# Masks turned by DMA instead of TensorE in a four-layer graph network: twelve in the first stage, ten among the sums

## The chip, the cores and the metric

The kernel runs on one core of a Trainium2 chip. The metric is the device time of one execution in microseconds (us). The time before is 2909.86 us, the median of three runs (2909.22 to 2911.19).

## The reference, cut to what matters

Four graph layers follow one another over N = 2708 nodes with 512 features each; every layer ends in a residual and a layer norm. All use the same adjacency matrix `adj` (2708 x 2708, int32, 0 or 1, symmetric by construction, with ones on the diagonal). The change touches only layer 0 and the way in which the adjacency comes into memory:

```python
Ab = A > 0
keep = Ab & (jnp.cumsum(Ab.astype(jnp.int32), axis=1) <= 64)    # first 64 neighbours of each row
nb_mean = (keep @ X) / jnp.maximum(keep.sum(axis=1), 1.0)
xj = jax.nn.leaky_relu(nb_mean @ W_nb.T + b_nb)
xi = jax.nn.leaky_relu(X @ W_line.T + b_line)
x = layernorm(x + xi + jnp.where(cnt > 0, xj, 0))
```

Layer 1 uses the whole mask instead of the first 64 neighbours (`mask @ x / deg`), layers 2 and 3 are attention with the same mask.

## The kernel before, in words

The rows are cut into NT = 22 tiles of P = 128; the last one has only `few` = 20 rows. One matrix `maskT` (128 x 22 x 2816, fp8, in on-chip memory) holds the transposed mask for all four layers. Each entry is a sign: 0 is no neighbour, one sign is a neighbour that is kept, the other a neighbour past the 64th.

**How one mask tile is made.** A "mask" is a block of 128 rows of `adj`. Its steps are:

- *load* (L270-L273): GpSimd (POOL) issues a DMA that reads 128 rows of int32 and writes bf16 into a tile `m`.
- *count* (L275-L277): one ScalarE (ACT) instruction over 2708 columns, with the row sum in `cnts`.
- *place* (L279-L286): VectorE (DVE) runs a scan along the row (L283) and multiplies (L286), in two halves in the first stage and in four quarters later.
- *turn*: the block is transposed. Before, there are two ways. `turn_here` (L288-L304) does it on TensorE (PE), in 22 transposes (L295) into PSUM, read by ACT as signs into `maskT` (L299). `turn` (L306-L307) does it by one DMA transpose, issued by SyncE (SP), into a bf16 tile `into`, which ACT reads as *signs* (L309-L315). Both end with a small DMA of the last rows, issued by POOL (L302, L314).

**The first stage** (L320-L369) loops over the 22 row tiles of x. For each tile PE multiplies by W_nb (the product called A here, `product` with `wnT`, L346), transposes the next tile of x into PSUM (L133), and multiplies by W_line (the product called B, L361). `keep_y` (L230) takes A apart: ACT copies the high half to `yH` (L231) and DVE subtracts for the low half `yL` (L236). B gets its bias (L363), a leaky ReLU (L195) and goes to memory by a POOL DMA (L365). ACT copies the transposed x out of PSUM (`xT`, L135); both products of the next tile need this copy. Product B has one PSUM buffer, which is free again when L363 has read it. Of the 22 masks, HERE = 14 are made in this stage (L265). The rule in L354 spreads them over the tiles from tile 2 on. They are loaded one ahead into three buffers `m` (L337). Their transposes go to PE in the written order: L350 puts the turn of a mask behind the next transposes of x. The order of PE in this stage is written out by hand (`pe`, L104); the other engines' instructions are put in order by the scheduler of the framework, which works with priorities, `issue_after` and its own estimates of time.

**The sums** (L373-L532) multiply the kept mask with `yH` and `yL`. The output tiles are taken in six blocks (two tiles, then five times four), and each block goes through 22 groups of PE instructions (L516), one for each j. ACT makes the operand `kT` of each group from `maskT` (L380), in two buffers. Behind each group one *step* of a generator is taken (L522). It runs through three parts: `other_masks` (L383) makes the remaining 8 masks, `weights1` the weights of layer 1, `vectors` those of the attention layers (L481). In `other_masks` a mask takes 11 steps: count, two empty ones, four quarters of place, at which the signs of the mask before are also made, two empty ones, then the turn and three more. The masks lie in two buffers, `spare` and `w`, which are zeroed and loaded one ahead (L389), and are turned into `weight2`. The layer norms of a finished block (`finish`, L430) run beside the groups of the next, on `rows` that SP loads. The 132 groups take 132 steps, the rest is run behind the loop (L531).

**Memory.** `yH` and `yL` (L212-L213) hold all 22 tiles of y in one piece each (128 x 22 x 512, fp32).

Of the kernel before, what the change touches and what calls it, by code (L numbers as in the profile page):

```python
# [2 lines left out]

# [6 lines left out]
F32 = mybir.dt.float32  # L10
F32R = mybir.dt.float32r
BF16 = mybir.dt.bfloat16
# [18 lines left out]
def kernel(  # L31
# [18 lines left out]
    def rows(t):  # L50
        return min(P, N - t * P)
# [151 lines left out]
    with ExitStack() as phase:  # L203
# [5 lines left out]
        gate = yp.tile([P, 1], F32, name="gate")  # L209
        nc.vector.memset(gate, -STEP / 2)  # L210
        weight2 = yp.tile([P, KD, D], F32, name="weight2")
        yH = yp.tile([P, NT, D], F32R, name="yH")  # L212
        yL = yp.tile([P, NT, D], F32R, name="yL")  # L213
        nc.gpsimd.memset(yH[:, NT - 1, :].bitcast(F32), 0.0)
        nc.gpsimd.memset(yL[:, NT - 1, :].bitcast(F32), 0.0)

        ps_tr = phase.enter_context(tc.tile_pool(name="ps_tr", bufs=2, space=PSUM))
        ps_mm = phase.enter_context(tc.tile_pool(name="ps_mm", bufs=1, space=PSUM))
# [9 lines left out]
        highs = {}  # L228

        def keep_y(t, n, pm):  # L230
            highs[t] = nc.scalar.copy(yH[:n, t, :], pm[:n])  # L231
            if t == LAST:
                low = slice(TWIN, TWIN + n)
                nc.scalar.copy(yL[low, t, :], pm[low])
                return nc.vector.tensor_sub(yH[low, t, :], pm[low], yL[low, t, :].bitcast(F32))
            return nc.vector.tensor_sub(yL[:n, t, :], pm[:n], yH[:n, t, :].bitcast(F32))  # L236

        def halves(j):

# [22 lines left out]

        HERE = NT - 8  # L265
        cuts = [(b, min(b + 4, NT)) for b in range(0, NT, 4)]
        cuts = cuts[-1:] + cuts[:-1]
        turns = [t for b in cuts for t in range(*b)]
# [10 lines left out]
        def place(i, m, places, part, of):  # L279
# [4 lines left out]
                                         places[:n, c0 - N * (part - 1) // of - 1:][:, :1] if part else -KEEP - 0.5,  # L284
                                         OP.add, OP.min)
            return nc.vector.tensor_mul(m[:n, c0:c1], m[:n, c0:c1], places[:n, :c1 - c0])  # L286

        def turn_here(i, m, psum, order=as_it_comes):  # L288
            t, n = turns[i], rows(turns[i])
            for g0 in range(0, NT, G):  # L290
                g1 = min(g0 + G, NT)
                ps = psum()
                for j in range(g0, g1):
                    w = rows(j)
                    order(nc.tensor.transpose(ps[:w, j - g0, :n], m[:n, j * P:j * P + w], identb[:n, :n]))  # L295
                parts = [(P, g0, min(g1, FULL))] + ([(rows(FULL), FULL, NT)] if g1 > FULL else [])
                for w, a, b in parts:
                    if a < b:
                        nc.scalar.activation(maskT[:w, a:b, t * P:t * P + n], ps[:w, a - g0:b - g0, :n], AF.Sign,  # L299
                                             saturate=False)  # L300
                if g1 == NT:
                    nc.gpsimd.dma_start(maskT[TWIN:TWIN + few, LAST, t * P:t * P + n],  # L302
                                        maskT[:few, LAST, t * P:t * P + n])
                yield  # L304

        def turn(i, m, into):  # L306
            nc.sync.dma_start_transpose(into, m)  # L307
# [12 lines left out]
        with ExitStack() as ph:  # L320
            st = ph.enter_context(tc.tile_pool(name="l0a", bufs=1))
            wnT, wlT = weight(), weight2
            room = [maskT[:, G + k, :4 * D].bitcast(F32) for k in range(2 * KD)]

            xs = rows_of(x)
            xTs = early(0, NT, lambda t, order=as_it_comes: transposed(ahead, ps_tr, xs(t), rows(t), "xT", order))

            transpose_weight(room[:KD], ps_tr, wnT, l0_w_nb, (nc.sync, nc.scalar))  # L330
            lows = {}
            for t in range(2):
                xT = xTs(t, order=pe)
                lows[t] = keep_y(t, P, product(xT, P, wnT, 0, pe))
            transpose_weight(room[KD:], ps_tr, wlT, l0_w_line)
            b_line = bias(bcast(l0_b_line, D))
            masks = early(1, HERE, lambda i: load_mask(i, st.tile([P, N], BF16, name="m", bufs=3)))  # L337
            masks(0)
            nc.gpsimd.memset(maskT[:, NT - 1, :], 0.0)
            nc.gpsimd.memset(maskT[:, :, N:], 0.0)  # L340
            counted = turned = 0
            for t in range(NT):
                n = rows(t)
                if t > 1:

                    lows[t] = keep_y(t, n, product(xTs(t, order=pe), n, wnT, 0, pe, sums() if t % 2 else None))  # L346
                xT = xTs(t)
                if t + 1 < NT:
                    xTs(t + 1, order=pe)
                while turned < counted - (t + 2 < NT):  # L350
                    for _ in turn_here(turned, masks(turned), lambda: sums(BF16, (P, G, P)), pe):
                        pass
                    turned += 1
                now = counted < min(HERE, -(-(t - 1) * HERE // (NT - 5)))  # L354
                if now:
                    m, places = masks(counted), st.tile([P, N // 2], BF16, name="places", bufs=1)
                    with tc.issue_after(highs[t].ins):
# [12 lines left out]

        with ExitStack() as ph:  # L373
# [9 lines left out]
            def other_masks():  # L383

                def room(i):
                    r = (ahead.tile([P, 2 * KD * (D + 2 * H)], BF16, name="w", tag="w", bufs=1) if i % 2 else
                         st.tile([P, 2 * KD * D], BF16, name="spare", tag="spare"))
                    m = r[:, :NT * P]
                    nc.gpsimd.memset(m[:, N:], 0.0)  # L389
                    load_mask(i, m)  # L390
                    return m, r[:, NT * P:NT * P + N // 4 + 1]

                got, left = {HERE: room(HERE)}, iter(())
                into = weight2.rearrange("p k c -> p (k c)").bitcast(BF16)[:, :NT * P].rearrange("p (t n) -> p t n", n=P)
                for i in range(HERE, NT):
                    if i + 1 < NT:
                        got[i + 1] = room(i + 1)
                    m, places = got.pop(i)
                    if i == HERE:
                        for _ in range(5):  # L400
                            yield
# [10 lines left out]
                    yield  # L412
# [93 lines left out]
            for i, b in enumerate(cuts):  # L506
                ts_ = range(*b)
                pa = {t: sums() for t in ts_}
                for j in range(NT):
                    if j + 1 < NT:  # L510
                        nxt, nxt_made = kept(b, j + 1)
                    elif i + 1 < len(cuts):
                        nxt, nxt_made = kept(cuts[i + 1], 0)
                    for t in ts_:
                        for y in halves(j):
                            nc.tensor.matmul(pa[t], kT[:, (t - b[0]) * P:(t - b[0] + 1) * P], y[:, j, :],  # L516
                                             start=(j == 0 and y is yH), stop=(j == LAST))
# [36 lines left out]
        with ExitStack() as ph:  # L554
            st = ph.enter_context(tc.tile_pool(name="l1b", bufs=2))
            for t in range(NT):
# [4 lines left out]
                for g0 in range(0, NT, G):  # L561
# [2 lines left out]
                    nc.scalar.copy(mf[:, :g1 - g0, :], maskT[:, g0:g1, t * P:(t + 1) * P])  # L564
                    for j in range(g0, g1):
                        for y in halves(j):
                            nc.tensor.matmul(pa, mf[:, j - g0, :], y[:, j, :],  # L567
                                             start=(j == 0 and y is yH), stop=(j == LAST))
                u = sm.tile([P, D], F32, name="u")
                nc.vector.scalar_tensor_tensor(u[:n], pa[:n], rdeg[:n, t:t + 1], z1, op0=OP.mult, op1=OP.add)  # L570
# [957 lines left out]
```

## Time and profile before

| What | Value |
|---|---|
| median of three runs | 2909.86 us |
| profiled execution, its own time | 2911.22 us |
| its span, first to last instruction | 2909.0 us |
| mean granted TensorE clock | 0.996 |
| DVE, ACT, POOL busy over the span | 68%, 52%, 9% |
| first stage, to the last product B (starts 203.25 us) | about 207 us |
| sums, to the last group of L516 (starts 467.97 us) | about 261 us |
| PE busy from 24 to 204 us, and from 204 to 468 us | 172.04 of 180, 255.87 of 264 us |

In the page and in the answers of the trace a line such as `L283 DVE TENSOR_TENSOR_SCAN` names the line of the kernel, the engine and the operation; then come the output and inputs, the shape and the number of instructions. A timeline line begins with the start and the length in us; in square brackets it has the time for which the engine stood idle before it, and what it waited for. A line with x8 is a run of eight instructions merged: an fp32 product of four matmuls shows as eight. Products overlap, so their pace is read from their starts.

### The profile page before, as it was taken

To read this page: it belongs to the slowest core of one execution; us is meant where nothing else is said; L and a number is where in the kernel's file an instruction comes from. 1 tells how busy PE (TensorE), PEld (TensorE's weight loads), DVE (VectorE), ACT (ScalarE), POOL (GpSimd) and SP (SyncE) were. 2 spreads that over 40 slices of the span, in tenths; PEclk is the share of its full clock that TensorE was granted. 3 is DMA by queue.
4 is the path that set the end of the run, shared out by engine and by line. 5 is a ranking of instruction groups with operands and counts; after the bars stand their busy time and mean duration, and the time that the engine had idled before them with its cause. 6 is when DMAs were issued, how large, how long until landed. Compare 5 with 4: busy or idle time off the path is not lost. (4 is left out here: it accounts for less than half of the span.)

```text
span 2909.0 us, 36145 instructions
## 1 busy us (share of the span) xinstructions
PE 2827.0 (97%) x14194; PEld 1576.5 (54%) x14194; DVE 1983.5 (68%) x2341; ACT 1501.7 (52%) x1749; POOL 247.5 (9%) x395
## 2 busy tenths in 40 slices
PE   8999999999999999999999999999999999999997
PEld 4457766458887434444466433444375555555555
DVE  6966737442334999999978999999954435435342
ACT  3546632122323999999955999999950000000001
POOL 1111110101110000000022000000200010100001
PEclk9999999999999999999999999999999999999999
DMA  5635536322222011111153111110171000000000
GB/s 134 129 86 121 139 110 176 112 65 93 77 75 78 27 37 37 35 46 47 34 155 107 37 37 40 47 45 34 35 179 42 4 29 11 26 15 16 15 22 21
DMA packets 145301, 187.33 MB, mean 64 GB/s; under 512 B 65791, under 2 KB 90692, under 8 KB 145122
## 3 DMA queue, kind: packets, MB, share of 16 engines
q1 hardware_dynamic: 115254, 123.27, 14.5%
q0 software_dynamic: 18864, 57.45, 7.0%
q10 hardware_dynamic: 11004, 4.22, 0.6%
q8 instruction: 114, 1.87, 0.3%
q14 instruction: 65, 0.53, 0.1%
HBM read 148.91 MB, written 44.65 MB: 67 GB/s over the span
## 5 line engine op out<-in xcount | busy, mean ns | idle before, releaser
L772 DVE SCALAR_TENSOR_TENSOR e<-v_bc,ucol,maskT 128x1408 f32<-128x1408 f32 (+3 forms) x804 | 1133.4, 1472 | 320.2 <-PE pn L1155 312.1
L801 ACT ACTIVATE c<-e,bcol 128x1300 fp8e4<-128x1300 f32 (+2 forms) x688 | 956.6, 1412 | 61.9 <-DVE e L772 16.7
L973 PE MATMUL po<-e,R 128*64 128x512 f32 (+3 forms) x4224 | 893.7, 548 | 25.9 <-DVE e L772 23.8
L973 PEld LDWEIGHTS po<-e,R 128*64 128x64 f32 (+1 forms) x4224 | 333.8, 136 | 552.7 <-issue 389.9
L1155 PE MATMUL pn<-e,R 128*128 128x512 f32 (+3 forms) x1056 | 403.0, 545 | 1.1 <-DVE lin L1175 0.4
L1155 PEld LDWEIGHTS pn<-e,R 128*128 128x128 f32 (+1 forms) x1056 | 183.9, 190 | 197.1 <-issue 181.5
L1105 ACT ACTIVATE w<-pl,b 128x256 f32<-128x256 f32 (+1 forms) x88 | 41.0, 466 | 370.9 <-PE pl L1103 370.9
L516 PE MATMUL acc<-yH,kT 128*128 128x512 f32 x484 | 194.5, 407 | 8.1 <-ACT kT L380 6.0
L567 PE MATMUL acc<-yH,mf 128*128 128x512 f32 x484 | 185.0, 389 | 0.0
L516 PE MATMUL acc<-yL,kT 128*128 128x512 f32 x462 | 181.1, 392 | 0.0
L567 PE MATMUL acc<-yL,mf 128*128 128x512 f32 x462 | 179.7, 389 | 0.0
L122 POOL TENSOR_TENSOR ln_rs<-ln_rs,half 128x1 f32<-128x1 f32 (+1 forms) x88 | 55.4, 630 | 1340.9 <-DVE ln_rs L121 1334.1
L694 PE MATMUL pm<-w,xT 128*128 128x264 f32 (+1 forms) x704 | 165.2, 388 | 2.8 <-DVE R L712 1.2
L259 PE MATMUL pm<-weight,xT 128*128 128x512 f32 (+1 forms) x344 | 156.7, 598 | 9.4 <-DVE u L363 8.0
L1103 PE MATMUL pl<-lin 128*128 128x256 f32 (+1 forms) x704 | 155.9, 376 | 3.4 <-DVE lin L1002 3.4
L1128 PE MATMUL pl<-lin,w 128*128 128x512 f32 x336 | 150.8, 593 | 0.0
L1103 PEld LDWEIGHTS pl<-lin 128*128 128x128 f32 x704 | 131.2, 193 | 34.6 <-issue 15.8
L694 PEld LDWEIGHTS pm<-w,xT 128*128 128x128 f32 (+1 forms) x704 | 129.7, 190 | 25.7 <-ACT xT L135 3.5
L564 ACT CAST mf<-maskT 128x1024 fp32r<-128x1024 fp8e4 (+1 forms) x66 | 64.5, 977 | 151.5 <-PE acc L567 148.2
L259 PE MATMUL pm<-w,xT 128*128 128x512 f32 x296 | 133.4, 593 | 3.3 <-ACT xT L135 2.1
L380 ACT ACTIVATE kT<-maskT 128x512 fp32r<-128x512 fp8e4 (+1 forms) x132 | 77.7, 593 | 103.8 <-PE acc L516 102.1
L873 PE MATMUL pd<-c,parts_c 128*12 128x384 fp8e4 (+2 forms) x2688 | 128.3, 307 | 0.0
(250 smaller groups left out, 2629.1 us busy)
## 6 DMA issues: line engine op xcount, KB each, us to landing
rows<-x_dram SPq DMA_DIRECT2D x63, 256.0 KB
v_bc<-v_dram SPq DMA_DIRECT2D x16, 704.0 KB
rows<-in_x_dram SPq DMA_DIRECT2D x42, 256.0 KB
x_dram<-u POOLq DMA_DIRECT2D x42, 256.0 KB, 2.4
v_bc<-v_dram SPq DMA_DIRECT2D x16, 650.0 KB
m<-in_adj_dram POOLq DMA_DIRECT2D x13, 677.0 KB, 7.1
r_dram<-u POOLq DMA_DIRECT2D x21, 256.0 KB, 2.3
rows<-r_dram SPq DMA_DIRECT2D x21, 256.0 KB
```

The lines of the kernel that those rows point to most:

```text
L259: order(nc.tensor.matmul(pm[:m], xT[:, k, :m], w[:, k, :], start=(k == 0), stop=(k == KD - 1)))
L380: made = nc.scalar.activation(kT[:, :w], maskT[:, j, b[0] * P:b[0] * P + w], AF.Relu, scale=-1.0)
L516: nc.tensor.matmul(pa[t], kT[:, (t - b[0]) * P:(t - b[0] + 1) * P], y[:, j, :], start=(j == 0 and y is yH), stop=(j == LAST))
L567: nc.tensor.matmul(pa, mf[:, j - g0, :], y[:, j, :], start=(j == 0 and y is yH), stop=(j == LAST))
L694: nc.tensor.matmul(pm[a][:m, :D // 2 + heads], xT[:, k, :m], w[:, k, a, :D // 2 + heads], start=(k == 0), stop=(k == KD - 1))
L772: self.made = nc.vector.scalar_tensor_tensor(e[:, :w], v[:, :w], ucol[:, j, h:h + 1], maskT[:, j, c0:c0 + w], op0=OP.max, op1=OP.mult)
L801: nc.scalar.activation(c[:, :w], e[:, :w], AF.Sigmoid, bias=bcol[:, j, h:h + 1], scale=STEP, saturate=False)
L873: pe(nc.tensor.matmul(p[32 * g:32 * g + 12, :c1 - c0], parts_c[:, j, h, :], c[:, c0:c1], start=(i == 0 and h == hs[0]), stop=(i == NT - 1 ...
L973: pe(nc.tensor.matmul(po[i][HO * k:HO * k + HO, :c1 - c0], R2[at, j, h * HO:(h + 1) * HO], e[at, a:a + c1 - c0], start=(i_ == 0), stop=(i_ ...
L1103: nc.tensor.matmul(pl[:, :w], self.lin1[:, k, f * P:(f + 1) * P], h[:, k, :w], start=(k == 0), stop=(k == KD - 1))
L1128: nc.tensor.matmul(pl[:n], gT[:, f, (t - t0) * P:(t - t0) * P + n], self.lin2[:, f, :], start=(f == 0), stop=(f == KF - 1))
L1155: nc.tensor.matmul(pn[k][:, :w], R2[at, j, k * P:(k + 1) * P], e[at, :w], start=(j == 0), stop=(j == NT - 1))
```

## The change

The change has five parts.

1. `turn_here` goes. All masks are turned by DMA transposes from SP, and ACT reads the signs from the bf16 tile that the DMA wrote.
2. HERE is 12 instead of 14: two masks move from the first stage to the sums, which now make ten.
3. The tiles into which the first ten masks of the first stage are turned lie in memory that y needs only at the end: `yH` and `yL` hold tiles 0 to 18 in one piece, and tiles 19 to 21 lie in a pair of tiles `end`. Until tile 19 these serve as two buffers for turned masks; before y is written there, the signs of the first ten must have been read. The last two masks are turned into the third buffer of `m` and the one after it.
4. The mask tiles are 2816 columns wide instead of 2708, with the tail (for the short mask the whole tile) zeroed by POOL before each load. The turn of a mask is written behind the transposes of x of the next tile, and the signs of a mask at the end of an iteration, when the next mask has been turned.
5. Among the sums the two empty steps ahead of the turn go: nine steps for a mask instead of eleven.

```diff
-        yH = yp.tile([P, NT, D], F32R, name="yH")
-        yL = yp.tile([P, NT, D], F32R, name="yL")
-        nc.gpsimd.memset(yH[:, NT - 1, :].bitcast(F32), 0.0)
-        nc.gpsimd.memset(yL[:, NT - 1, :].bitcast(F32), 0.0)
+        END = NT - 3
+        starts, ends = [yp.tile([P, END, D], F32R, name=name) for name in ("yH", "yL")], []
+
+        def end_tile(dtype):
+            return yp.tile([P, 3 * D * 4 // mybir.dt.size(dtype)], dtype, name="end", tag="end", bufs=2)
+
+        def part_of(i, t):
+            return starts[i][:, t, :] if t < END else ends[i][:, (t - END) * D:(t - END + 1) * D]
+
+        yH, yL = (partial(part_of, i) for i in range(2))
...
-        HERE = NT - 8
+        HERE = NT - 10
...
-        def turn_here(i, m, psum, order=as_it_comes):
...
-            masks = early(1, HERE, lambda i: load_mask(i, st.tile([P, N], BF16, name="m", bufs=3)))
+            def mask_tile():
+                return st.tile([P, NT * P], BF16, name="m", bufs=3)
+
+            def mask_rows(i):
+                m = mask_tile()
+                nc.gpsimd.memset(m[:, N:], 0.0)
+                if rows(turns[i]) < P:
+                    nc.gpsimd.memset(m, 0.0)
+                return load_mask(i, m)
+
+            def turned_tile(i):
+                if i >= HERE - 2:
+                    return mask_tile().rearrange("p (t n) -> p t n", n=P)
+                return end_tile(BF16)[:, :NT * P].rearrange("p (t n) -> p t n", n=P)
+
+            masks = early(1, HERE, mask_rows)
+            intos = {}
+
+            def turn_next(i):
+                intos[i] = turned_tile(i)
+                turn(i, masks(i), intos[i])
+
+            def signs_of(i):
+                for _ in signs(i, intos.pop(i)):
+                    pass
...
-            counted = turned = 0
+            counted = turned = signed = 0
             for t in range(NT):
                 n = rows(t)
+                if t == END:
+                    while signed < HERE - 2:
+                        signs_of(signed)
+                        signed += 1
+                    ends[:] = [end_tile(F32R) for _ in range(2)]
+                    for y in (yH, yL):
+                        nc.gpsimd.memset(y(LAST).bitcast(F32), 0.0)
...
-                while turned < counted - (t + 2 < NT):
-                    for _ in turn_here(turned, masks(turned), lambda: sums(BF16, (P, G, P)), pe):
-                        pass
+                while turned < counted:
+                    turn_next(turned)
                     turned += 1
...
                     counted += 1
+                while signed < (HERE if t == NT - 1 else turned - 1):
+                    signs_of(signed)
+                    signed += 1
...
                     for _ in left:
                         pass
-                    yield
-                    yield
                     turn(i, m, into)
```

The other lines of the diff only write `yH(t)` for `yH[:, t, :]` and the like.

More of the change, by code (lines that the diff above doesn't have):

```diff
@@ L1 @@
 from contextlib import ExitStack, nullcontext
+from functools import partial
 from itertools import chain
@@ L230, in keep_y @@
         def keep_y(t, n, pm):
-            highs[t] = nc.scalar.copy(yH[:n, t, :], pm[:n])
+            highs[t] = nc.scalar.copy(yH(t)[:n], pm[:n])
             if t == LAST:
                 low = slice(TWIN, TWIN + n)
-                nc.scalar.copy(yL[low, t, :], pm[low])
-                return nc.vector.tensor_sub(yH[low, t, :], pm[low], yL[low, t, :].bitcast(F32))
-            return nc.vector.tensor_sub(yL[:n, t, :], pm[:n], yH[:n, t, :].bitcast(F32))
+                nc.scalar.copy(yL(t)[low], pm[low])
+                return nc.vector.tensor_sub(yH(t)[low], pm[low], yL(t)[low].bitcast(F32))
+            return nc.vector.tensor_sub(yL(t)[:n], pm[:n], yH(t)[:n].bitcast(F32))
         def halves(j):
@@ L286, in place @@
             return nc.vector.tensor_mul(m[:n, c0:c1], m[:n, c0:c1], places[:n, :c1 - c0])
-        def turn_here(i, m, psum, order=as_it_comes):
[L289 to L303, printed above, removed]
-                yield
         def turn(i, m, into):
@@ L410, in other_masks @@
                         pass
-                    yield
-                    yield
                     turn(i, m, into)
@@ L515 @@
                         for y in halves(j):
-                            nc.tensor.matmul(pa[t], kT[:, (t - b[0]) * P:(t - b[0] + 1) * P], y[:, j, :],
+                            nc.tensor.matmul(pa[t], kT[:, (t - b[0]) * P:(t - b[0] + 1) * P], y(j),
                                              start=(j == 0 and y is yH), stop=(j == LAST))
@@ L566 @@
                         for y in halves(j):
-                            nc.tensor.matmul(pa, mf[:, j - g0, :], y[:, j, :],
+                            nc.tensor.matmul(pa, mf[:, j - g0, :], y(j),
                                              start=(j == 0 and y is yH), stop=(j == LAST))
```

## The prediction

> **What bounds the kernel now.** I read the page's busy times, then a table of the stages' windows, then the timeline of one tile of the first stage and of one mask among the sums, and last the waits of both stretches. The page says that TensorE (PE) is busy nearly throughout, so time taken off PE should come off the end, and time in which PE waits is added to it:
>
> ```profile
> span 2909.0 us, 36145 instructions
> PE 2827.0 (97%) x14194; PEld 1576.5 (54%) x14194; DVE 1983.5 (68%) x2341; ACT 1501.7 (52%) x1749; POOL 247.5 (9%) x395
> ```
>
> The change touches only the first 500 us. In the table of windows the columns are start:end, length, then busy us of PE, weight loads, VectorE (DVE), ScalarE (ACT) and GpSimd, granted clock, DMA share and GB/s:
>
> ```profile
> core 0: us, PE busy (x) PEld busy (x) DVE busy (x) ACT busy (x) POOL busy (x), PEclk, DMA share, GB/s
> 100.00:120.00 20.00, 19.46 (x90) 10.31 (x89) 19.76 (x19) 13.95 (x18) 3.63 (x6) 1.00 0.62 125
> ...
> 320.00:360.00 40.00, 38.93 (x168) 30.66 (x166) 30.48 (x53) 25.61 (x37) 8.03 (x12) 1.00 0.57 153
> ```
>
> In the first stage, in a stretch with a mask in every tile, PE and DVE are both full: less PE work alone can win little there. Among the sums PE alone is full. One tile of the first stage:
>
> ```profile
> 101.56 3.60 PE L259 MATMUL pm<-w,xT 128*128 128x512 f32 x8
> ...
> 102.23 2.95 DVE L283 TENSOR_TENSOR_SCAN places<-m,over 128x1354 bf16<-128x1354 bf16 x1
> ...
> 105.19 0.59 ACT L231 CAST yH<-pm 128x512 fp32r<-128x512 f32 x1 [2.66 <-PE pm L259]
> ...
> 105.43 1.49 PE L295 MATMUL acc<-identb,m 128*128 128x128 bf16 x22
> ...
> 105.68 0.59 ACT L135 COPY xT<-ps_tr 128x512 f32<-128x512 f32 x1
> ...
> 106.17 2.55 ACT L277 ACTIVATE m<-m,gate 128x2708 bf16<-128x2708 bf16 x1
> ...
> 106.85 3.70 PE L259 MATMUL pm<-weight,xT 128*128 128x512 f32 x8
> ...
> 108.71 2.64 ACT L299 ACTIVATE maskT<-acc 128x1024 fp8e4<-128x1024 bf16 x4
> ```
>
> PE's starts give the tile: product with W_nb 3.43 (to 104.99), transpose of x 0.44, a mask's 22 transposes 1.42, product with W_line 3.54; 8.83 in all, 7.4 without the mask. ACT's order is: high half of y, xT, count, and the signs, whose PE transposes are long done. And a mask among the sums:
>
> ```profile
> 223.71 3.48 SPq L307 DMA_TRANSPOSE weight<-spare  x1
> ...
> 229.02 1.06 ACT L312 ACTIVATE maskT<-weight 128x1024 fp8e4<-128x1024 bf16 x1 [2.09 <-DMA weight<-spare]
> ...
> 229.13 0.19 POOL L389 MEMSET spare<- 128x108 bf16 x1 [19.99 <-DMA weight<-spare]
> ...
> 230.43 0.50 PE L516 MATMUL acc<-yH,kT 128*128 128x512 f32 x1 [1.62 <-ACT kT L380]
> ```
>
> This is the pattern that decides. The transpose takes 5.3 us from its issue (223.71) to landing (229.0); ACT came to its signs 2.09 us too early and stood; the kT that PE needs lay behind, and PE lost 1.62 us.
>
> **What the Trainium skill says.** "PSUM — Partial Sum Buffer", Engine vs sequencer instructions: the queues of ScalarE, VectorE and GpSimd are strictly first in, first out. The trace agrees: the kT of 230 was held by a sign that it doesn't need. "VectorE: DVE Perf Modes", The three transpose paths: a 128x128 bf16 block costs 390 ns on TensorE and 1309 ns by DMA. In bulk both are cheaper here, 1.49/22 = 0.07 us and 5.3/22 = 0.24 us, but DMA stays the slower by 3.5 times. "DMA: Bandwidth & Descriptors", Issuing engines are not separate DMA queues: all DMAs interleave on the same 16 engines. The eight transposes agree: seven landed after 5.2 to 5.4 us, the one issued at 317.51, with row loads behind it, after 7.1.
>
> **The change, part by part.** I use the order of instructions on each engine in the built kernel, and durations from this profile.
>
> *PE transposes out of the first stage:* 13 x 1.42 + 0.75 (the 20-row mask) = 19.2 us off PE. *Two masks moved to the sums:* 2 x (2.95 + 0.86 + 3.03 + 0.87) = 15.4 us off DVE here; there 2 x 4 x (1.63 + 0.51) = 17.1 us, beside DVE's slack (30.5 of 40 busy), so nothing by itself, but 2 x 2.5 us of count in ACT's queue, each of which cost PE 0.21 among four-tile sums (six waits of PE on "ACT kT" after 245 us): 0.4.
>
> *The new wait.* Twelve masks now fall to tiles 2,3,4 | 6,7 | 9,10,11 | 13,14 | 16,17. In the built ACT order the first one or two sign groups of each mask stand ahead of the high half and xT of a following tile. After the last mask of each group they also stand ahead of the next group's first count. So sign of the last mask -> high, xT, count -> DVE's scans of the next group -> DMA transpose -> sign is one closed chain, with PE's next product behind xT. Its price: two sign groups 1.75, high 0.5, xT 0.5, count 2.55 and its 0.19 read: 5.5. The first mask on DVE: scan 2.98, product 0.79, scan 3.07, product 0.79, with leaky and subtraction (0.61 + 0.60) between: 8.9. Each further one 9.0 (the same with the addition, 0.72). Issue to landing 5.35. So 28.8 us for a group of two and 37.8 for three, where PE alone would want 3 x 7.4 = 22.2 and 4 x 7.4 = 29.6. In the profile of before mask 2 leaves DVE at 67.5; turned by DMA it lands at 72.9, and from there 28.8 + 37.8 + 28.8 + 28.8 = 124.2 brings the last sign of the stage to 197.1. Behind it: signs, high and xT 2.8, two W_nb products, one W_line product and transposes 11.3, so PE would begin the last W_line product at 211.2, against 203.25 now: **+7.9**. The saving of 19.2 is inside this: it turns into PE waiting.
>
> Each us on a landing counts five times. A mask load (677 KB, 6.1 to 7 us to land) now starts when a transpose lands and reaches into the next one: +0 to +1.75 each (5.35 to 7.1), I take 0.2: **+1**.
>
> *SP's queue:* ten transposes, 3.3 us of SP each, wait for DVE ahead of x's row loads; three row buffers give each load two tiles, some 15 us: nothing, else up to 3 us once or twice. *Memory of the end tiles:* signs of mask 9 must be read before y of tile 19 is written; that is some 20 us ahead: nothing. *Zeroing (L389's like):* 12 x 0.19 us and one of 2.5 on idle GpSimd: nothing.
>
> *Nine steps for eleven among the sums.* A step is one group of PE (1.82 us for four tiles). From a mask's count to its first sign lay 13 steps: 326.90 to 351.58 = 24.7 us. The removed two leave 11: 20.4. From count to landing the eight masks took 17.4, 17.3, 20.5, 16.9, 23.3, 18.7, 24.7, 16.7 us. The longest are those whose scans meet the layer norms of the block before. At 20.4 those of 23.3 and 24.7 are late by 2.9 and 4.3; kT is made some 1.2 us ahead, so PE loses 1.7 and 3.1. With ten masks over five blocks I expect three such, mean 2.4: 7.2, of which the before kernel paid none; the first block's wait of 1.62 grows by two short steps of 0.92: +1.8 at most. Row loads can also sit behind two transposes on SP. Nothing gets faster here (PE's work is unchanged). Range 1 to 14; I take **+6**, the 0.4 above included.
>
> *Tail:* 142 steps for 140; 132 fit into the loop, so two more vector steps (0.69 + 0.69 us of DVE each) run into the next stage, where DVE is busy 26 of 30 us: 0 to 2.8, I take **0**. Past that the built order is the same instruction by instruction.
>
> Sum: 7.9 + 1 + 6 + 0 = 15 us. The profiled execution took 2911.2 (span 2909.0 and 2.2 around it), 1.4 above the median of the three runs; so 2926 like it, and 2909.9 + 15 = **2925** as a median.
>
> **The rivals.** (1) *ACT is never early* and the stage gains. If DVE's last product ends at least 5.4 us before PE finishes the next W_nb product, the sign group finds its data and the chain is open. Then DVE's 15.4 or PE's 19.2 us less shows: about -14 in the first stage and +3 among the sums, 2899. For it: ACT is busy only 13.95 of 20. Against it: DVE is busy 19.76 of 20, so it ends late in every tile. (2) *A wash:* ACT waits, but runs of one group overlap better than my chain, the stage ends as before and the sums add 2 to 3: 2912. (3) *Contention:* each transpose in the first stage takes 7.1 us, five on the chain: +9, and the sums at their upper end, +14: 2909.9 + 7.9 + 9 + 14 = 2941. That the change doesn't do what it says is excluded by the built order: no mask transpose is left on PE.
>
> **How the numbers follow.** 0.2% (5.8 us) is about what a measurement can tell from no change. Forecast 2925: 0.66; contention 2941: 0.14; wash 2912: 0.11; faster 2899: 0.09. So slower 0.80, same 0.11, faster 0.09. The range 2908 to 2940 takes in the wash and the bounds of the forecast, and leaves out the gain and the worse half of contention.
>
> **What would show it.** Right: in the first stage waits "ACT maskT <- DMA" of 3 to 10 us, some ten of them, PE's busy share falling to about 0.82, last W_line product near 211; among the sums three or more such waits with PE waiting for kT behind. Wrong: no ACT wait on the transposes, DVE full, PE idle only for DVE's u. If the stage ends before 200, the closed chain was wrong.

## The result, and the profile after

The changed kernel takes **2948.82 us**, the median of four runs (2945.49 to 2949.82), beside 2910.53 for the kernel before. The ratio is 1.0128 with a 95% interval of [1.0111, 1.0146]: 38 us slower, where 15 had been forecast and the range ended at 2940. The profiled execution is the fastest of the four, 2945.49, which is 34.3 us over that of before. First the page's totals:

```profile
span 2943.2 us, 35606 instructions
PE 2827.3 (96%) x13886; PEld 1565.1 (53%) x13886; DVE 1988.0 (68%) x2349; ACT 1502.0 (51%) x1749; POOL 253.3 (9%) x410
```

PE has 308 instructions fewer and is busy as long as before (2827.0): the 19.2 us of mask transposes are gone, and something made the other matmuls longer by as much. The windows of the first stage show where (same columns as in the prediction):

```profile
core 0: us, PE busy (x) PEld busy (x) DVE busy (x) ACT busy (x) POOL busy (x), PEclk, DMA share, GB/s
60.00:110.00 50.00, 41.64 (x103) 18.18 (x101) 34.73 (x32) 21.12 (x32) 8.77 (x17) 0.93 0.80 151
110.00:160.00 50.00, 38.88 (x93) 17.08 (x92) 32.71 (x30) 25.91 (x33) 7.40 (x15) 0.90 0.78 161
```

The same two windows in the kernel before:

```profile
60.00:110.00 50.00, 46.72 (x220) 24.66 (x219) 45.86 (x39) 28.54 (x40) 9.08 (x15) 1.00 0.57 122
110.00:160.00 50.00, 48.13 (x221) 25.60 (x220) 45.86 (x40) 28.57 (x40) 8.32 (x14) 1.00 0.59 122
```

No engine is full any more, and the granted clock has fallen from 1.00 to 0.93 and 0.90. What they wait for, by ScalarE and by TensorE (total us, times, longest):

```profile
ACT maskT L301 <- DMA end<-m: 73.4, 10, 10.0
...
ACT maskT L301 <- DMA m<-m: 14.9, 2, 9.3
```

```profile
PE pm L266 <- DVE u L382: 12.9, 7, 3.6
PE pm L266 <- ACT xT L136: 12.2, 5, 6.5
PE acc L266 <- ACT xT L136: 8.4, 4, 3.6
```

All twelve masks make ACT stand, 88.3 us in all. Before, PE waited 0.7 us for xT in this stage and 8.0 for u (the tile into which DVE adds the bias to the W_line product, which frees the product's PSUM buffer). One such wait in the timeline, at the end of a group of three masks:

```profile
103.47 0.86 DVE L293 TENSOR_TENSOR m<-m,places 128x1354 bf16<-128x1354 bf16 x1
...
104.48 5.96 SPq L296 DMA_TRANSPOSE end<-m  x1
...
110.53 0.53 SPq L174 DMA_DIRECT2D rows<-in_x_dram  x1
114.03 2.00 ACT L301 ACTIVATE maskT<-end 128x1024 fp8e4<-128x1024 bf16 x2 [9.38 <-DMA end<-m]
115.94 0.57 ACT L238 CAST yH<-acc 128x512 fp32r<-128x512 f32 x1
116.40 0.59 ACT L136 COPY xT<-ps_tr 128x512 f32<-128x512 f32 x1
...
116.88 2.56 ACT L284 ACTIVATE m<-m,gate 128x2708 bf16<-128x2708 bf16 x1
117.04 5.49 PE L266 MATMUL pm<-w,xT 128*128 128x512 f32 x6 [6.53 <-ACT xT L136]
```

DVE's product ends at 104.3, the transpose goes out at once, ACT stands at the sign until 114.03, and only then come the high half, xT and the next count; PE starts behind xT, 6.53 us late. That is the predicted chain, link by link. Two things were not predicted: the landing takes 9.55 us instead of 5.35 (a mask load of 677 KB, asked for at 101.44, runs beside it), and PE's product then runs slowly (5.49 us for six matmuls of eight; 6.48 for all).

Three marks tell the stages apart in every run below: the start of the last matmul of the last W_line product, the start of the last copy u of the sums, and the span. The difference of the first two is here called the sums. Medians are beside the kernel before in the same series (2910 to 2912).

| Kernel | last product | last u | sums | span | median | ratio, interval |
|---|---|---|---|---|---|---|
| before | 206.3 | 470.1 | 263.8 | 2909.0 | 2910 to 2912 | 1 |
| after | 230.7 | 504.6 | 273.9 | 2943.2 | 2948.8 | 1.0128 [1.0111, 1.0146] |
| 1 signs late | 203.0 | 477.0 | 274.0 | 2917.9 | 2916.1 | 1.0019 [1.0012, 1.0027] |
| 2 cast on ScalarE | 237.7 | 514.4 | 276.7 | 2951.7 | 2942.0 | 1.0105 [1.0088, 1.0122] |
| 3 no reloads | 224.6 | 495.8 | 271.2 | 2932.6 | 2934.9 | 1.0077 [1.0058, 1.0097] |
| 4 PE turns 12 | 202.9 | 480.0 | 277.1 | 2917.5 | 2914.8 | 1.0016 [1.0010, 1.0023] |
| 5 all DMA, 14 | 239.0 | 501.5 | 262.5 | 2940.9 | 2938.7 | 1.0098 [1.0082, 1.0115] |
| 6 both repairs | 196.7 | 471.1 | 274.4 | 2910.2 | 2916.0 | 1.0017 [1.0008, 1.0027] |
| 7 both, 14 masks | 221.8 | 484.4 | 262.6 | 2923.1 | 2917.9 | 1.0030 [1.0020, 1.0040] |
| 8 PE turns 12, signs a step later | 200.8 | 471.2 | 270.4 | 2907.9 | 2913.0 | 1.0010 [1.0003, 1.0017] |
| 9 as 7, store first | 211.5 | 474.1 | 262.6 | 2914.4 | 2915.8 | 1.0014 [1.0004, 1.0023] |
| 10 as 6, store first | 200.0 | 472.4 | 272.4 | 2910.9 | 2913.1 | 1.0002 [0.9994, 1.0011] |
| 11 after, store first | 229.5 | 503.6 | 274.1 | 2940.6 | 2946.7 | 1.0121 [1.0103, 1.0138] |
| 12 as 10, signs a step later | 208.4 | 481.5 | 273.1 | 2921.3 | 2908.8 | 0.9996 [0.9988, 1.0004] |
| 13 before, 9 steps | 208.6 | 483.9 | 275.3 | 2922.3 | 2923.4 | 1.0044 [1.0027, 1.0061] |
| 14 PE turns 12, 10 steps | 202.6 | 477.3 | 274.7 | 2918.8 | 2919.7 | 1.0027 [1.0015, 1.0040] |

A warning for reading it: single executions of one kernel lay up to 19 us apart (number 9: 2907.31 to 2926.69; number 12: 2904.84 to 2923.27, the highest of its 14 being the profiled one). The marks come from one execution each; the verdicts are taken from the ratios. From before to after, the first stage brings 24.4 us, the sums 10.1, the tail (what follows the last u) nothing (2438.6 us against 2438.9). That is the 34.2 us between the two spans; the other 4 us between the medians are not placed in a stage, since the profiled execution of after is its fastest.

### The profile page after: what moved, and what is told of

Read it like the earlier page. It is cut to its first block, busy times and chain, and to the rows that moved or that the text cites. A ratio compares the mean times of both kernels' runs of the same rounds, so it can differ in the third digit from the quotient of the medians.

```text
span 2943.2 us, 35606 instructions
## 1 busy us (share of the span) xinstructions
PE 2827.3 (96%) x13886; PEld 1565.1 (53%) x13886; DVE 1988.0 (68%) x2349; ACT 1502.0 (51%) x1749; POOL 253.3 (9%) x410
## 3 DMA queue, kind: packets, MB, share of 16 engines
q8 instruction: 111, 1.82, 0.3%
## 5 line engine op out<-in xcount | busy, mean ns | idle before, releaser
L1175 PEld LDWEIGHTS pn<-e,R 128*128 128x128 f32 (+1 forms) x1056 | 183.9, 190 | 197.1 <-issue 181.5
L536 PE MATMUL acc<-yH,kT 128*128 128x512 f32 x418 | 169.7, 406 | 13.1 <-ACT kT L402 10.1
L536 PE MATMUL acc<-yL,kT 128*128 128x512 f32 x418 | 163.3, 391 | 0.0
L587 PE MATMUL acc<-yH,mf 128*128 128x512 f32 x418 | 162.7, 389 | 0.0
L587 PE MATMUL acc<-yL,mf 128*128 128x512 f32 x418 | 162.6, 389 | 0.0
L266 PE MATMUL pm<-w,xT 128*128 128x512 f32 x296 | 139.7, 616 | 14.7 <-ACT xT L136 13.7
```

The source lines that it names most:

```text
L266: order(nc.tensor.matmul(pm[:m], xT[:, k, :m], w[:, k, :], start=(k == 0), stop=(k == KD - 1)))
L587: nc.tensor.matmul(pa, mf[:, j - g0, :], y(j), start=(j == 0 and y is yH), stop=(j == LAST))
L1175: nc.tensor.matmul(pn[k][:, :w], R2[at, j, k * P:(k + 1) * P], e[at, :w], start=(j == 0), stop=(j == NT - 1))
```

## The experiments

**1. Signs behind the copies.** In the changed kernel ACT takes the signs behind this tile's count, or its xT copy where there is no count.

```diff
-                        count(counted, m)
+                        copied[:] = [count(counted, m)]
...
-        nc.scalar.copy(dst[:, :, :n], ps[:, :, :n])
+        copied[:] = [nc.scalar.copy(dst[:, :, :n], ps[:, :, :n])]
...
                 while signed < (HERE if t == NT - 1 else turned - 1):
-                    signs_of(signed)
+                    with tc.issue_after(copied[0].ins):
+                        signs_of(signed)
```

> The changed kernel, with one thing altered: in stage 1, ScalarE takes a mask's signs behind this tile's count (or, where there is none, behind its copy of xT), not ahead of the first tile's copy. My theory: the last first-layer product is late because ScalarE stands at a sign that waits for a landing (5.2 to 9.6 us), while the tile's copies and the next count are queued behind it. With the copies and the count ahead, most of the 24 us of stage 1 comes back, less the 4.9 us of the start, which this leaves: W_line's last product at 197 to 205 us, the whole about 2921 us (2915 to 2930). Rival: the landings themselves hold the stage, through the buffers that they free and the row loads behind them on SyncE's queue, whatever ScalarE does meanwhile: the last product stays past 220 us, the whole at 2940 to 2950. Rival: a wait for a sign that is still ahead of the next tile's copies keeps about half of it: 2930 to 2937.

2916.1: 33 us of the 38 are gone (25 between the two profiled spans), and the last product comes at 203.0. The waits of the stage, ACT and then PE (the second view has no line of xT above 0.7 us):

```profile
ACT maskT L303 <- DMA end<-m: 19.2, 6, 6.9
...
ACT maskT L303 <- DMA m<-m: 2.8, 1, 2.8
```

```profile
PE pm L268 <- DVE u L384: 17.1, 10, 3.6
...
PE pm L268 <- ACT xT L138: 0.7, 1, 0.7
```

The transposes themselves are no quicker (two of them land only 10.3 and 11.0 us after their issue); what was moved is only who stands behind them. So the loss of the first stage was the order on ACT, and neither rival (the landings hold the stage by themselves; half of it stays) gives this number.

**2. The identity's cast on ScalarE.** The trace after has a second surprise in the first 12 us, on GpSimd and on VectorE:

```profile
2.70 2.46 POOL L352 MEMSET maskT<- 128x2816 fp8e4 x1
5.08 2.46 POOL L333 MEMSET m<- 128x2816 bf16 x1
7.47 2.10 POOL L353 MEMSET maskT<- 128x2376 fp8e4 x1
```

```profile
2.68 6.97 DVE L65 CAST identb<-ident 128x128 bf16<-128x128 f32 x1 [1.43 <-POOL ident masks.py:199]
2.82 6.83 DVE L100 TENSOR_REDUCE groups<-ident 128x32 f32<-128x128 f32 x2
```

In the kernel before this cast took 0.53 us, and ended just behind a short zeroing of GpSimd (1.70 to 2.22):

```profile
1.77 0.53 DVE L64 CAST identb<-ident 128x128 bf16<-128x128 f32 x1 [0.52 <-POOL ident masks.py:199]
```

Here it lasts until GpSimd's three zeroings end at 9.57; the zeroing that the change adds (L333, the whole tile of the short mask) put the row of them together right there. DVE's copies of the first weights stand behind, and PE waits 3.1 us for one ("PE ps_tr L146 <- DVE w L147"). The first product starts at 13.44 instead of 10.21.

```diff
-    nc.vector.tensor_copy(identb, ident)
+    nc.scalar.copy(identb, ident)
```

> The changed kernel, with the cast of the identity to bf16 at the start taken by ScalarE in place of VectorE; the zeroing on GpSimd stays as it is. The trace after shows VectorE's cast lasting 6.97 us beside GpSimd's row of zeroing. Theory A, the cast alone stands in the way: stage 1 starts 4.9 us earlier and all of it reaches the end, 2944 us against 2949. Theory B, anything VectorE does in that stretch is held, the reduction for the weights next, so that PE waits as long as before: 2949, no change. Theory C, stage 1 has slack for the start further on: the start is earlier, the last product is not: 2947 to 2949.

In the trace VectorE is free again:

```profile
2.68 0.64 DVE L100 TENSOR_REDUCE groups<-ident 128x32 f32<-128x128 f32 x2 [1.43 <-POOL ident masks.py:199]
```

so the reduction was only queued behind the cast (theory B falls). The first product comes 1.6 us earlier, not 3.2, since PE now waits 1.5 us for a row load. The median is 2942.0, but its interval overlaps that of after, and the profiled execution, 2953.5, is the highest of its four: a gain of a few us is likely, its size is not shown.

**3. Without the masks' reloads.** Nine of the twelve loads are left out; the tiles are filled with ones.

```diff
                 nc.gpsimd.memset(m[:, N:], 0.0)
+                if i > 2:
+                    nc.gpsimd.memset(m[:, :N], 1.0)
+                    return m
```

> The changed kernel, but of the first stage's masks only the first three are read from memory; for the other nine GpSimd fills the tile with ones (2.5 us each), so the counts and sums of those rows are not the reference's. The order of the engines, the DMA transposes and the signs stay. Theory, a mask's load beside a transpose lengthens its landing: all landings fall to 5.2 to 5.5 us, the last of a group too (now 5.7 to 9.6), and stage 1 shortens by about 10 us: 2938 us (2935 to 2942). Rival, a transpose behind another on SyncE's queue, or the row loads beside it, lengthens it: the last of each group stays at 7 to 9 us, and the whole at 2946 to 2950.

2934.9, and the interval lies below that of after: 14 us. The transpose of 104.48 in this kernel, SP's queue and ACT:

```profile
101.33 3.40 SPq L296 DMA_TRANSPOSE end<-m  x1
```

```profile
107.52 2.00 ACT L301 ACTIVATE maskT<-end 128x1024 fp8e4<-128x1024 bf16 x2 [6.04 <-DMA end<-m]
```

Landing in 6.2 us instead of 9.55, and SP holds it for 3.40 us instead of 5.96. The last transposes of the first four groups now land after 6.0, 6.2, 6.3 and 6.2 us, before 8.9, 9.55, 6.15 and 7.2: the load beside it is what made the long ones long. The 0.7 to 0.9 us by which they still exceed 5.35 are not the load's, so the theory's 5.2 to 5.5 for all was too low. Together the last transposes of the five groups land 6.8 us sooner, and the last product comes 6.1 us earlier. The spans of the two profiled executions differ by 10.6 us, not 14: 2.7 of these lie in the sums and 1.8 in the tail, which the edit does not touch.

**4. The counts alone.** The kernel before with twelve masks in the first stage and nine steps, turned by PE.

```diff
-        HERE = NT - 8
+        HERE = NT - 10
...
                         pass
-                    yield
-                    yield
                     turn(i, m, into)
```

> The kernel before, with the two counts of the change alone: twelve masks in stage 1, still turned by TensorE, and ten among the sums with nine steps each, turned by DMA as before. It tells the part of the sums apart. Theory: stage 1 is 4 to 6 us shorter (two masks less to turn, count and sign), the sums are 8 to 11 us longer, as in the changed kernel, since ten masks wait closer on one another: 2915 us (2911 to 2920). Rival, the sums carry most of the loss: 2930 or more. Rival, the counts cost nothing, and the sums' 10 us in the changed kernel came over from the late end of stage 1: 2904 to 2909.

2914.8, the theory's number, with the first stage 3.4 us shorter and the sums 13 longer; the theory had 4 to 6 and 8 to 11, and this execution lies 4.7 us above its median. The loss of the sums is there without any change in the first stage's turning.

**5. The turning alone.** The changed kernel with HERE = NT - 8 and the two empty steps put back.

> The changed kernel, with the counts of before: fourteen masks in stage 1 and eight among the sums with eleven steps each; all turned by DMA, signs where the change put them. It tells the turning from the counts. Theory: stage 1 is set by the closed chain from a group's last sign round to the next group, and a mask more inside a group only takes the place of part of a tile: worked through the queues with the landings as measured, the last product comes at the same time with 14 masks as with 12, within 2 us. The sums fall back by their 10 us: 2939 us (2934 to 2944). Rival: each mask turned by DMA in stage 1 costs its 9 us on ScalarE's path, so two more cost 18 us there and win 10 in the sums: 2957. Rival: the counts were the loss: 2915 or less.

2938.7, the theory's number; the sums are back at 262.5. But the marks say that the numbers of the stages were not quite mine: its last product comes 8.3 us later than after's, where the theory had 2 and the rival 18. This execution was its highest of four and after's the lowest, so a part of the 8 us is scatter; a mask more in a group costs between nothing and half of its 9 us.

**6. Both repairs.** Number 1, with the signs held back by one mask more (`turned - 1 if counted == HERE else counted - 2`), and number 2.

> The changed kernel with both repairs: the signs behind the tile's own copies and behind the count of the mask two further on, and the identity's cast on ScalarE. If the two losses of stage 1 are separate, they add: 2916 less the 5 to 7 us of the start, 2910 us (2906 to 2914), which is the kernel before within the measurement. If the start only fills slack once the closed chain is gone: 2916.

2916.0, not distinguishable from number 1: with the chain open, the start's repair and the later signs together gain nothing that shows; what each does with the chain open was not tried. The trace has its first stage end at 196.7, 9.6 us before that of the kernel before, and the sums lose 10.6; it is the second lowest of its twelve executions, so a part of the 9.6 is scatter.

**7. Both repairs and the old counts.**

> Both repairs, and the counts of before (fourteen masks in stage 1, eight among the sums, eleven steps). Worked through the queues, stage 1 with 14 masks and late signs ends 4 us earlier than in the kernel before (ScalarE no longer waits at a sign, TensorE has no mask to turn), and the sums are those of before: 2906 us (2901 to 2911). Rival: with 14 masks ScalarE and VectorE have no room left, and stage 1 ends with that of before or later: 2911 to 2916.

2917.9: the rival, and above its range. The waits of GpSimd and VectorE name the next bound:

```profile
POOL m L333 <- DMA end<-m: 85.3, 11, 15.7
...
DVE u L384 <- DMA r_dram<-u: 17.9, 3, 9.3
```

GpSimd stands at the next mask's buffer, which is free only when its transpose has landed; the store of u (`r_dram`) is behind it on GpSimd's queue, and DVE's next u needs that store's buffer.

**8. Signs a step later among the sums**, in number 4.

```diff
-                        next(left, None)
+                        if part:
+                            next(left, None)
```

> The kernel before with twelve masks in stage 1 and ten among the sums at nine steps (measured at 2914.8), and among the sums a mask's first piece of sign taken one step later. Theory: the sums lose their 10 us where ScalarE stands at a sign whose landing is late, with the next kT behind it, since with nine steps VectorE has no slack ahead of the transpose; a step later takes most of these waits away: 2909 to 2912. Rival: it is the rest of a step (the kT copies, the scans and the count set closer), and later signs leave it: 2914 to 2916.

2913.0: its interval overlaps that of number 4. Between the two expectations, inconclusive.

**9, 10, 11. The store ahead of the next request**, in numbers 7 and 6 and in the changed kernel.

```diff
-            masks = early(1, HERE, mask_rows)
+            masks = early(0, HERE, mask_rows)
...
-            masks(0)
+            masks(1)
...
                     counted += 1
+                    masks(min(counted, HERE - 1))
```

> The kernel with both repairs and 14 masks (measured at 2917.9), in which GpSimd asks for the next mask behind the tile's store of u, not ahead of it. In that kernel's trace the request waits for a transpose to land (85 us in all, up to 15.7), the store of u stands behind it on GpSimd's queue, and VectorE's next u waits for the store (17.9 us, three times). Theory: with the store ahead, these waits go, and stage 1 ends 12 to 18 us earlier: 2905 us (2900 to 2911). Rival: the wait was for the u buffers of a stage bound elsewhere (TensorE's clock, the landings of 14 transposes and 14 loads that share the transfers), and the stage stays: 2914 to 2919.

> The same with twelve masks in stage 1 and ten among the sums (measured at 2916.0 with the request ahead of the store). Its waits for the store were small, so theory: 2 us or less are won, 2914 to 2916; the rest over the kernel before is the sums. Rival: the request held the stores here too: 2908 to 2912.

> The changed kernel with that one alteration alone, the next mask asked for behind the store of u. Theory: ScalarE's closed chain sets stage 1 there, and GpSimd's queue is beside it: 2946 to 2952, no change. Rival: part of the loss was the stores held behind the requests: 2935 to 2943.

Number 11 is as the theory says: in the changed kernel GpSimd's queue is beside the path. Number 9 is a miss of the theory, and its rival's number: the waits for the store fall only from 17.9 to 14.3 us (the longest 5.5), the last product comes 10 us earlier in the trace (number 7's execution lay 7 us above its median), but the median is only 2 us lower, within the intervals. With fourteen masks all turned by DMA the stage stays no better than with PE turning them; why PE still waits there for u, 14 times and 23.1 us, is not settled. Number 10 lies between its two expectations and is not distinguishable from the kernel before (1.0002), nor, by the intervals, from number 6.

**12. Everything**: number 10 with number 8's edit.

> The twelve-mask kernel with late signs, the cast on ScalarE and the store first (measured at 2913.1, against 2911.8 for the kernel before), with the first piece of sign among the sums a step later as well. Theory: the sums lose about 10 us where ScalarE stands at signs whose landing is late, and a step later takes part of that away (2 us where it was tried with TensorE turning, its trace 7): 2906 to 2911, at or a little under the kernel before. Rival: the sums' loss is in steps set too close for VectorE, and later signs leave it: 2912 to 2914.

2908.8, ratio 0.9996: the same as the kernel before, and no better. The number is the theory's, its reason is not shown: the sums of this trace, 273.1 us, are no shorter than number 10's 272.4. No version of the change beats the kernel before.

**13, 14. The sums: steps or masks?** The kernel before with nine steps and still eight masks; number 4 with one of the two empty steps put back.

```diff
-                    yield
-                    yield
                     turn(i, m, into)
```

> The kernel before with nine steps for a mask among the sums in place of eleven; fourteen masks in stage 1 and eight among the sums, as before. If the sums' loss comes of steps set closer: eight tenths of it, 2917 to 2921. If it comes of the two masks more: no loss, 2908 to 2912.

> The kernel before with twelve masks in stage 1 and ten among the sums, at ten steps each in place of nine (measured at 2914.8 with nine). If the loss comes of steps set closer, half of the sums' loss goes: 2909 to 2912. If it comes of the two masks more (each brings 2.5 us of count and 3.1 us of signs to ScalarE and 8.6 us of scans to VectorE, beside kT): 2914 to 2916 still.

Number 13 decides one half: eight masks at nine steps lose 13 us (11.5 in the sums by the marks), so the closer steps are enough by themselves. Its waits among the sums behind the first block, ACT and PE:

```profile
ACT maskT L312 <- DMA weight<-w: 9.7, 2, 5.2
```

```profile
PE acc L514 <- ACT kT L380: 7.9, 8, 3.9
```

In the kernel before these are 0.5 us once and 1.3 us in six. Number 14 misses both expectations: ten steps lose as much (the sums 274.7), and the median is no lower than number 4's. The added step does what it was meant to do: ACT stands at signs for 7.5 us over the sums, 14.4 in number 4, and PE waits 6.7 us for kT, 14.1 there. But at the end of two blocks ACT's copies of the sums now stand behind a count (until 314.9) and behind a late sign (until 360.9), and PE waits 7.3 us for u instead of 3.0. Where in a block a mask's steps fall matters as well as the slack; how to place them best stays open.

## Why the prediction was wrong, step by step

Direction and mechanism hold; the size fell out of the range because three terms were too small: the landings, the zeroing at the start and the steps among the sums.

- **The new wait, the closed chain: right.** Signs that wait for a landing, with the high half, xT and count behind them: number 1 removes it and 33 us with it. With the signs late, DMA turning (2916.1) costs hardly more than PE turning the same twelve masks (number 4, 2914.8). The count of waits (twelve, 3 to 10 us) and PE's share (121.88 of 150 us, 0.81, forecast 0.82) are as written. The groups' cycles, from the sign of one group's last mask to that of the next, measured 31.9, 40.1, 29.6 and 29.1 us, forecast 28.8, 37.8, 28.8, 28.8.
- **"+0 to +1.75 each ... I take 0.2": the step that failed most.** The last transposes of the five groups landed 8.94, 9.55, 6.15, 7.18 and 5.76 us after their issue, so 3.6 + 4.2 + 0.8 + 1.8 + 0.4 = 10.8 us over 5.35 where I took 1, and three lie past the 7.1 that I had set as the worst. Number 3 shows the cause of most of it (6.8 us of the 10.8): mask loads that start when a transpose lands and run beside the next. I had the overlap and priced it from one overlap with row loads in the kernel before.
- **"Zeroing on idle GpSimd: nothing": failed.** GpSimd was idle, but VectorE's cast stood until its zeroings ended, and the first product started 3.2 us late. The third W_nb product started at 35.86 instead of 30.95, 4.9 us late: the other 1.7 us are the first product, which took 5.38 us instead of 3.70. Number 4, without these zeroings, has such a first product too (5.50), so that part is not the zeroing's. With the landings the sum for the last sign of the stage becomes 197.1 + 4.9 + 10.8 = 212.8, and it starts at 212.81. That it closes so well is luck: for the first wait and then group by group it misses by +0.7, -1.1, +1.5, -1.0 and -0.1 us. What the repair wins in the whole is not settled (number 2: a few us; number 6: nothing visible).
- **The first stage together.** Forecast +7.9 and 1; measured +24.4 (the last product starts at 227.66, forecast 211.2). From PE's side the same sum reads: its waits grew from 16.1 to 44.1 us (+28.0), the mask transposes left (-19.2), and seven products ran slowly (+13.7, below): 22.5 of the 24.4. That last term was in no step of mine. It is partly the same time as the chain's, since the chain does not run over PE, so it is not added to the terms above.
- **"Nine steps for eleven among the sums", +6, range 1 to 14: right in mechanism, low.** It measured +10.1. Over the whole of the sums ACT stood at four signs for 12.6 us (3.9 in the first block, then 8.7 in three), before at two for 2.6; PE waited 15.7 us for kT and u, before 7.9. Most of the other 2.3 us are the clock: the sums have two stretches of 3.41 us at half clock (from 255.79 and 341.12), before one. The forecast had three late signs at a mean of 2.4 for PE, and undercut its own terms: 7.2 and 0.4, with up to 1.8 in the first block, make 7.6 to 9.4, and it took 6. Nor do its figures give the 20.4 us for eleven steps: 24.7 less two steps of 1.82 is 21.1. Number 13 shows that the closer steps suffice, number 14 that my picture of slack, a step for a step, is too simple.
- **SP, memory of the end tiles, tail: nothing, right.** The tail moved by 0.3 us.
- **The rivals.** Contention, at 2941 with 0.14, was nearest: it named both the landings and the sums' upper end, and had 7.1 us for each of five landings. "ACT is never early" is what number 1 makes of the change, and even that gave 2916 and not 2899: where ACT no longer holds the stage, DVE's u does, and the sums' loss stays.

PE's wait for kT over the whole of the sums, in the kernel before and in the changed one:

```profile
PE acc L516 <- ACT kT L380: 6.0, 9, 1.6
```

```profile
PE acc L536 <- ACT kT L402: 12.7, 13, 3.4
```

## What to carry to other kernels

When a transfer takes the place of an engine's work, look first at the in-order queue that reads its result: the same twelve transposes cost 33 us with the readers ahead of the next tile's copies and almost nothing behind them. A landing time taken from a stretch in which the transfer ran alone is a lower bound (5.35 us here, 8.9 and 9.55 beside a load); if the freed buffer starts a load at that moment, take the pair. And work on an idle engine can hold another engine up: here 7 us of zeroing on GpSimd held a cast on VectorE for 6.97 us.

## What the runs showed of the hardware

**A short wait of TensorE can cost more than its length.** In the first stage of the changed kernel seven products last 5.1 to 6.7 us instead of 3.6 to 3.7, the first one and six behind a wait of 3.1 to 6.5 us; the trace of the kernel before has none there. Two of them:

```profile
84.16 5.40 PE L266 MATMUL acc<-w,xT 128*128 128x512 f32 x8 [3.15 <-ACT xT L136]
...
171.20 6.71 PE L266 MATMUL pm<-weight,xT 128*128 128x512 f32 x8 [3.56 <-DVE u L382]
```

The Trainium skill, "TensorE: Matmul & The Clock Gate", Part 1: The HAM clock gate, says that after an idle window of some 3.4 us the array runs at half its clock until it has been busy for about as long, and that the windows run freely. The runs agree on the half clock and on the free windows: half clock for 3.4 us costs 1.7, and 5.40 - 3.70 is 1.70. In the first stage of the changed kernel, behind its first product, the half clock comes in stretches of 3.41 or 6.83 us that begin at 71.47, 85.12, 115.84, 146.56, 170.46 and 201.18 us, that is 4, 9, 9, 7 and 9 times 3.41 us apart. They do not agree on how idle a window must be. The first product above starts at 84.16, and the clock falls in the middle of it, at 85.12; in the window before, PE was busy for 0.96 of 3.41 us (columns as above; the granted clock is the third from the end):

```profile
81.71:85.12 3.41, 0.96 (x2) 0.49 (x3) 1.29 (x2) 3.03 (x4) 0.91 (x2) 1.00 0.30 38
85.12:88.54 3.42, 3.42 (x6) 1.35 (x5) 1.86 (x1) 3.28 (x5) 0.00 (x0) 0.50 0.91 173
```

In number 10 a wait of 1.91 us that lies wholly in one window (62.82 to 66.24) brought a product of 5.40. In number 2 a wait of 3.72 us, from 145.57 to 149.29, cost nothing beyond itself: the border of two windows cuts it into 1.80 and 1.92 us, and the product behind it took 3.70:

```profile
143.95:147.37 3.42, 1.62 (x4) 0.38 (x2) 3.38 (x3) 1.10 (x2) 1.28 (x3) 1.00 1.03 258
147.37:150.78 3.41, 1.49 (x4) 0.78 (x5) 2.62 (x4) 2.68 (x5) 0.62 (x2) 1.00 0.76 118
```

Laid on such a grid from 18 to 480 us, all sixteen traces show the same, with the ends of matmuls as the profile models them: a window at full clock with more than 2.0 us of idle PE is always followed by half clock, one with less than 1.5 us never, and in between both occur. What a wait costs thus depends on where it falls on a grid that lies differently in each execution, which fits the scatter between executions of one kernel; that it is the cause of the scatter is not shown.

**A cast held for 7 us by zeroing on another engine** (number 2). The skill, "SBUF — State Buffer", SBUF: two separate sides, says that VectorE in a two-port mode and GpSimd take a shared pair of ports as an exclusive lock, for the whole instruction. The trace agrees that the cast stands and that the reduction, once the cast is elsewhere, runs in 0.64 us beside the same zeroings; but it stood not for one instruction but for three in a row, 6.97 us. That this cast runs in such a mode no run here shows.
